# Layer 0's weighted sums over the keys: four column tiles of 32 instead of two of 64

## The chip, the cores and the metric

The kernel runs on one core of one Trainium2 chip. The metric is the device time of one execution in microseconds (us). Five engines of the core take part: TensorE (PE in the profile; its weight loads are listed apart as PEld), VectorE (DVE), ScalarE (ACT), GpSimd (POOL) and SyncE (SP), which issues most of the DMA transfers.

## The reference

The input x has 8 images of 512 channels and 32 x 32 = 1024 positions. Two attention layers follow each other. The core of layer 0, cut to what matters here:

```
h = group_norm(x);  q, k, v = split(qkv_w @ h + qkv_b)          # 8 heads of 64 channels
q, k, v = fake_quant(q), fake_quant(k), fake_quant(v)            # one 8-bit scale for each whole tensor
w = softmax(einsum('bct,bcs->bts', q * scale, k * scale))        # 64 head-images, 1024 x 1024
a = einsum('bts,bcs->bct', w, v)                                 # weighted sums over the keys s
x = x + proj_w @ a + proj_b
```

Layer 1 is a group norm and an attention with a single head of 512 channels on the result, with projections wq, wk, wv and wp, and again a residual sum.

## The kernel before

**First stage (0 to about 600 us).** Image by image the kernel normalises x, multiplies it with the qkv weights and writes q, k and v to device memory, because the quantization needs the extremes of the whole tensors before any score can be computed.

**Second stage (about 600 us to the end).** Layer 0's attention is a generator, `attention()`. Its work is cut into 512 *units* (b, j, hf, s): image b, pair of heads j, half hf of the 1024 queries (512 each), key tile s of 128 keys. What a unit passes through:

- `scores(u)`: two matmuls, one for each head of the pair, give the scores of 128 keys against 512 queries in a two-bank PSUM tile `st`. Each has a contraction of 64 channels, so the two heads share the array by rows (64*128 in the profile). ACT takes the exponential into `pt`.
- `split(u)`: `pt` (32-bit) is split into two 16-bit parts, `two[:, 0]` (a cast, on ACT or POOL) and `two[:, 1]` (the rest, by a subtraction on DVE). Sums over both parts are close to 32-bit sums.
- `over_keys(us)`: the weighted sums, `av` in the profile. The stationary operand is v of the unit's key tile, 128 keys x 128 channels, of which 64 belong to each head of the pair; the moving operand is a part of the exponentials, 128 keys x 512 queries, for each head. The result for a pair is one PSUM bank `av`, head 0 in partitions 0 to 63 and head 1 in 64 to 127, accumulated over the 8 key tiles and both parts.
- `totals(us)`: the row sums, `sm` in the profile, with a stationary operand of ones, 128 x 32 (`ones16`). Four matmuls for a unit (two parts x two heads) write four partition strips of 32 of one PSUM bank, strips of `QUAD` = 32.

For image 0 every fourth key tile is an exception (`plain(b, s)`): its exponentials stay 32-bit, and `over_keys` and `totals` multiply them in two and two 32-bit matmuls. That is 16 units of the 512.

A step of the generator, `advance()`, takes four units through `over_keys` and `totals` and calls `scores` for four later ones. The order inside the step has three forms. The usual one is `over_keys` of four units and then `totals` of the four. A `dense` step does two units at a time: `over_keys`, `totals`, `scores`, `over_keys`, `totals`. A `late` step is similar, with `scores` between the first `over_keys` and `totals`. The rest of the work (the projection of layer 0, `pj`; layer 1's products `g`, `v2ps`, `s`, `o`) comes from a second generator, `others()`, which calls `advance()` at its own places. In the second stage all matmuls pass through `mm`, which chains each to the one before, so PE runs in program order:

```
part = lhsT.shape[-1] / P if lhsT.shape[-1] in (32, 64) else 1.0
...
pe.t += math.prod(rhs.shape[1:]) * 1.677e-3 * part
```

The same helper advances the planner's clock `pe.t`. From the planner's estimates the order of the chores on DVE and ACT is set when the program is built. A matmul with 32 stationary columns counts half of one with 64.

Each step of `over_keys` and `totals` keeps its PSUM bank in the pool `ps_v` (two banks): one `av` and one `sm`. `finish` copies both out on ACT after the last key tile of a half.

Of the kernel before, what the change touches and what calls it, by code (L numbers as in the profile page):

```python
# [58 lines left out]
def attn_pair_kernel(  # L59
# [101 lines left out]
    def awaits(t):  # L161

        pe.t = max(pe.t, t + 0.1)
# [41 lines left out]
    def mm(ps, lhsT, rhs, **kw):  # L205
        ins = nc.tensor.matmul(ps, lhsT=lhsT, rhs=rhs, **kw).ins  # L206
        part = lhsT.shape[-1] / P if lhsT.shape[-1] in (32, 64) else 1.0
        if rhs.dtype in (BF, F16, F32R):
            part *= 0.25 * lhsT.shape[0] / P
        pe.t += math.prod(rhs.shape[1:]) * 1.677e-3 * part  # L210
        if last_mm[0] is not None:
            tc.add_manual_dep(ins, last_mm[0].name, IN_ORDER, reason="order")
        last_mm[0] = ins
# [90 lines left out]
    with ExitStack() as fast:  # L304
# [4 lines left out]
        def av_bank(name):  # L309
            return ps_v.tile([P, 512], F32, tag="v", name=name)  # L310
# [447 lines left out]
        HALF = (slice(0, CH), slice(CH, P))  # L758

        QUAD = P // 4  # L760
# [33 lines left out]
        def plain(b, s):  # L794
            return b == 0 and s % 4 == 3
# [54 lines left out]
        def attention():  # L850
# [8 lines left out]
            pts, parts, avs, sms, rss, ready = {}, {}, {}, {}, {}, {}  # L859
# [57 lines left out]
            def need(u):  # L917

                while u not in ready:
                    e, name = (act, "cast") if u not in at_hand else (dve, "sum")  # L920
                    e.begin(next(i for i, c in enumerate(e.chores) if c[0] == name))

            def over_keys(us):
                need(us[-1])
                awaits(ready[us[-1]])
                pe.t += 0.12
                for u in us:
                    b, j, hf, s = units[u]
                    if s == 0:
                        avs[b, j, hf] = av_bank(f"av_{b}_{j}_{hf}")  # L930
                    if plain(b, s):
                        for i, r in enumerate(HALF):
                            mm(
                                avs[b, j, hf][r, :], lhsT=vfs[j][:, s // 4, r],
                                rhs=parts[u][:, i, :], start=False, stop=(s == NT - 1),
                            )
                        continue
                    for w in range(2):
                        for i, r in enumerate(HALF):
                            mm(  # L940
                                avs[b, j, hf][r, :], lhsT=pairs[b, j][2][:, s, r],
                                rhs=parts[u][:, w, i, :], start=(s == 0 and w == 0),
                                stop=(s == NT - 1 and w == 1),
                            )

# [61 lines left out]
            for u in range(0, len(units), 4):  # L1007
                b, j, hf, s = units[u]
# [17 lines left out]
                if late:  # L1026
                    over_keys((u, u + 1))
                    two(scores, u + 6)
                    totals((u, u + 1))
                    over_keys((u + 2, u + 3))  # L1030
                    totals((u + 2, u + 3))
                    two(split, u + 6)
                    two(scores, u + 8)
                elif dense:
                    over_keys((u, u + 1))
                    totals((u, u + 1))
                    two(split, u + 6)
                    two(scores, u + 8)
                    over_keys((u + 2, u + 3))
                    totals((u + 2, u + 3))  # L1040
                else:
                    over_keys(range(u, u + 4))
                    totals(range(u, u + 4))
                    two(split, u + 6)
                    two(scores, u + 8)
# [995 lines left out]
```

## Time and profile before

| | |
|---|---|
| Median of 3 runs | 2625.35 us (2622.46 to 2626.37) |
| The profiled execution's own time | 2624.97 us |
| Its span, first to last instruction | 2623.2 us |
| Mean granted TensorE clock | 0.995 |
| Busy: PE, PEld, DVE, ACT, POOL | 97%, 67%, 71%, 53%, 7% of the span |
| PE busy in 740 to 2408 us of the span | 1652.44 of 1668 us |
| `av` in 16-bit: matmuls, weight loads | 1984, 1984 |
| `sm` in 16-bit: matmuls, weight loads | 1984, 1984 |

The span leaves out what lies before the first and after the last instruction, 1.8 us here. The profile models the ends of matmuls, and matmuls overlap: a 16-bit one with 512 columns is listed with a duration of about 380 ns, while the next one on the same columns of the array starts after 216 ns. The time that a group of matmuls takes from the array is therefore read from where it starts to where the next group starts. In the profile a shape like 128*64 gives the rows and the columns of the array that a matmul occupies.

### The profile page before, as it was taken

Reading aid. Unit: us, or ns where it says so; the run is one execution under the profiler, and the core shown is the slowest. Engines: PE = TensorE matmul, PEld = TensorE weight load, DVE = VectorE, ACT = ScalarE, POOL = GpSimd, SP = SyncE. Lnnn points to the kernel's source line nnn. Section 1 sums busy time; section 2 is a strip of 40 time slices with the busy share of each in tenths; the row PEclk is TensorE's granted clock in tenths of the full one; section 3 lists DMA queues with packets and bytes.
Section 4 is the critical chain, followed back from the end, with each engine's and each line's share of the span. In section 5 each row is a group of like instructions: output and inputs, shape, how many; then the busy total and the mean of one; then the engine's idle time right before and its main releaser. Section 6 shows DMA issues by size and latency. Waiting matters only on the chain.

```text
span 2623.2 us, 34796 instructions
## 1 busy us (share of the span) xinstructions
PE 2556.4 (97%) x13686; PEld 1755.6 (67%) x13686; DVE 1864.0 (71%) x2675; ACT 1390.1 (53%) x1750; POOL 193.4 (7%) x160
## 2 busy tenths in 40 slices
PE   7899999998989999999999999999999999999998
PEld 4788888882236765775677576757766775677687
DVE  7866666558767777877776777778777776776544
ACT  3333333326866674766566566746665665664121
POOL 0000000001210001000100010010001000100000
PEclk9999999999999999999999999999999999999999
DMA  4433233333311123223212322322232123212211
GB/s 172 149 121 117 108 114 128 121 129 105 130 66 53 58 93 113 63 76 108 94 46 77 121 90 61 101 83 84 80 106 94 52 77 117 85 45 82 93 37 38
DMA packets 154942, 241.79 MB, mean 92 GB/s; under 512 B 26512, under 2 KB 92048, under 8 KB 153232
## 3 DMA queue, kind: packets, MB, share of 16 engines
q1 hardware_dynamic: 124064, 181.50, 21.0%
q10 hardware_dynamic: 30704, 57.97, 6.5%
q8 instruction: 109, 1.79, 0.3%
q14 instruction: 65, 0.53, 0.1%
HBM read 152.59 MB, written 86.28 MB: 91 GB/s over the span
## 4 chain that ended last, share of the span: by engine, by line
PE 87%; DVE 6%; issue 2%; ACT 2%; DMA 2%; POOL 0%; ACTq 0%; SPq 0%; DVEq 0%; POOLq 0%
PE s L206 15%; PE o L206 14%; PE qkps L206 13%; PE pj L206 8%; PE av L206 8%; PE v2ps L206 7%; PE vps L206 7%; PE g L206 7%; PE st L206 4%; PE sm L206 4%; DVE two L91 1%; ACT pt L91 1%; DMA raw<-q_d 1%; PE fold L206 0%; DVE acc L91 0%
## 5 line engine op out<-in xcount | busy, mean ns | idle before, releaser
L91 ACT ACTIVATE pt<-st,esc 128x1024 f32<-128x1024 f32 x496 | 526.9, 1115 | 356.6 <-PE st L206 331.7
L91 DVE TENSOR_TENSOR two<-pt,two 128x1024 f16<-128x1024 f32 x496 | 598.3, 1222 | 139.8 <-POOL two L906 111.0
L91 ACT CAST two<-pt 128x1024 f16<-128x1024 f32 x358 | 362.3, 1055 | 9.0 <-issue 6.5
L906 POOL CAST two<-pt 128x1024 f16<-128x1024 f32 x128 | 167.9, 1312 | 1557.0 <-PE sm L206 1036.0
L206 PE MATMUL av<-two,v 128*64 128x512 f16 x1984 | 246.1, 383 | 0.2 <-DVE two L91 0.2
L206 PE MATMUL s<-g,h 128*128 128x256 f32 x1024 | 234.1, 381 | 0.0
L206 PE MATMUL pj<-ao,wp 128*128 128x512 f32 x512 | 223.6, 595 | 0.0
L206 PEld LDWEIGHTS s<-g,h 128*128 128x128 f32 x1024 | 192.8, 190 | 31.9 <-issue 4.3
L206 PEld LDWEIGHTS <-v 128*64 128x64 f16 x1984 | 98.2, 109 | 133.9 <-issue 66.4
L206 PE MATMUL st<-q,k 64*128 64x512 bf16 x1024 | 162.0, 382 | 23.2 <-ACT pt L91 12.0
L206 PE MATMUL s<-g,sums 128*128 128x256 f32 x768 | 178.4, 381 | 0.2 <-DVE p L91 0.2
L206 PEld LDWEIGHTS pj<-ao,wp 128*128 128x128 f32 x512 | 96.1, 190 | 121.3 <-issue 114.1
L206 PE MATMUL o<-p,v 128*128 128x256 f32 x768 | 175.2, 382 | 1.0 <-DVE p L91 1.0
L206 PEld LDWEIGHTS o<-p,v 128*128 128x128 f32 x768 | 144.3, 190 | 27.1 <-issue 5.7
L206 PEld LDWEIGHTS s<-g,sums 128*128 128x128 f32 x768 | 144.7, 190 | 24.2 <-issue 4.6
L206 PE MATMUL sm<-two,ones 128*32 128x512 f16 x1984 | 137.8, 383 | 1.0 <-ACT rs L91 1.0
L91 ACT ACTIVATE u_ring<-qkps,qkbt 128x512 f32<-128x512 f32 x89 | 60.9, 685 | 140.9 <-PE qkps L206 131.2
L206 PE MATMUL qkps<-half,w_high 128*128 128x512 f32 x480 | 130.5, 394 | 0.0
L206 PEld LDWEIGHTS <-k 64*128 64x128 bf16 x1024 | 33.9, 94 | 143.4 <-issue 139.2
L206 PE MATMUL qkps<-half,w_mix 128*128 128x512 f32 x480 | 129.5, 392 | 0.0
L206 PE MATMUL qkps<-half,w_low 128*128 128x512 f32 x480 | 129.4, 391 | 0.0
L206 PE MATMUL g<-h,wa 128*128 128x256 f32 x512 | 120.6, 383 | 1.6 <-DVE h L91 1.6
(209 smaller groups left out, 3854.1 us busy)
## 6 DMA issues: line engine op xcount, KB each, us to landing
rs<-rs_d SPq DMA_DIRECT2D x80, 256.0 KB
x<-in_x_dram SPq DMA_DIRECT2D x32, 512.0 KB
q_d<-wa SPq DMA_DIRECT2D x32, 512.0 KB
k_d<-wa SPq DMA_DIRECT2D x32, 512.0 KB
raw<-q_d SPq DMA_DIRECT2D x32, 512.0 KB
raw<-k_d SPq DMA_DIRECT2D x32, 512.0 KB
v_d<-v_ring SPq DMA_DIRECT2D x32, 512.0 KB
x_d<-h SPq DMA_DIRECT2D x64, 256.0 KB
```

Source lines behind the costliest of these rows:

```text
L91: ins = self.latest = op(*args, **kw).ins
L206: ins = nc.tensor.matmul(ps, lhsT=lhsT, rhs=rhs, **kw).ins
L906: copy(two[:, 0], pt)
```

## The change

In `over_keys`, the loop over the two halves of the pair's 128 channels becomes a loop over four quarters of 32 channels. Quarters 0 and 1 belong to head 0, quarters 2 and 3 to head 1, so the moving operand of quarter i is `parts[u][:, w, i // 2, :]`. Each quarter writes its own strip of 32 partitions of the same bank. The path of the 16 `plain` units is untouched, and so are `totals` and `scores`.

```
                     for w in range(2):
-                        for i, r in enumerate(HALF):
+                        for i in range(4):
+                            r = slice(i * QUAD, (i + 1) * QUAD)
                             mm(
                                 avs[b, j, hf][r, :], lhsT=pairs[b, j][2][:, s, r],
-                                rhs=parts[u][:, w, i, :], start=(s == 0 and w == 0),
+                                rhs=parts[u][:, w, i // 2, :], start=(s == 0 and w == 0),
                                 stop=(s == NT - 1 and w == 1),
                             )
```

`av` then has 3968 16-bit matmuls of 128*32 and as many weight loads, where it had 1984 of 128*64. For the planner nothing changes in sum: four times a quarter is two times a half. PE's program grows by 3968 instructions, and the order of the instructions on DVE and ACT differs in a handful of neighbouring places; on SP and POOL it is the same.

## The prediction

> **What bounds the kernel now.** I began with the busy shares in the stretch in which layer 0's attention of images 1 to 7 runs among the other products, 740 to 2408 us, as the windows view has it (span, then busy us and count of each engine, clock, DMA share, GB/s):
>
> ```profile
> 740.00:2408.00 1668.00, 1652.44 (x9540) 1098.70 (x9539) 1247.14 (x1578) 1036.32 (x1288) 154.20 (x117) 1.00 0.25 81
> ```
>
> PE is idle for 1668.00 - 1652.44 = 15.6 us, under 1%. DVE has a quarter to spare and ACT over a third. So PE's own order of matmuls is the time here, and what it takes from the array can be saved. The chain that ended last agrees: the page gives PE 87% of it. In the costliest groups (count, then busy us and mean ns of one) the two that matter are
>
> ```profile
> L206 PE MATMUL av<-two,v 128*64 128x512 f16 x1984 | 246.1, 383 | 0.2 <-DVE two L91 0.2
> L206 PE MATMUL sm<-two,ones 128*32 128x512 f16 x1984 | 137.8, 383 | 1.0 <-ACT rs L91 1.0
> ```
>
> Same count, same moving size, same mean, and yet `sm` fills little over half the time of `av`: four `sm` matmuls run side by side, and two of `av`. Per matmul `av` costs 246.1 / 1984 = 124 ns and `sm` 69 ns. If the change only doubled the count at 69 ns, `av` would take 3968 x 69 ns = 276 us, 30 us more. Whether that reading holds is the question, so I went to the chain in order of time (start us, us, what), once through a dense step and once through a usual one:
>
> ```profile
> 1000.15 0.98 PE av L206 x8
> 1001.13 0.55 PE sm L206 x8
> 1001.68 0.54 PE st L206 x4
> ...
> 1032.82 0.54 PE st L206 x4
> 1033.36 1.85 PE av L206 x16
> 1035.20 0.98 PE sm L206 x16
> 1036.18 0.54 PE st L206 x4
> ```
>
> Call *wave* the matmuls that run side by side: two of `av` or `st`, four of `sm`. Eight more `av` matmuls, four waves, cost 1.85 - 0.98 = 0.87 us, so a wave is 0.217 us. Eight more `sm` matmuls, two waves, cost 0.98 - 0.55 = 0.43 us, 0.215 us a wave. I use 0.216. What is left of a group is the same for both: 0.98 - 4 x 0.216 = 0.116 us for `av`, 0.55 - 2 x 0.216 = 0.118 for `sm`, 0.108 for `st`. Every group pays some 0.115 us whatever its length. That fixed part, not dearer waves, is why short `sm` groups average 69 ns.
>
> Is the fixed part paid for a new bank, for new data, or for a new division of the array? Image 0 answers, in the timeline of PE (start us, us with overlaps, then the form):
>
> ```profile
> 656.82 0.62 PE L206 MATMUL av<-two,v 128*64 128x512 f16 x4
> 657.28 1.02 PE L206 MATMUL av<-aside,vf 128*64 128x512 f32 x4
> 658.23 0.40 PE L206 MATMUL sm<-two,ones 128*32 128x512 f16 x4
> 658.46 1.02 PE L206 MATMUL sm<-aside,ones 128*32 128x512 f32 x4
> ```
>
> From 16-bit to 32-bit operands at an unchanged 128*64, two waves last 657.28 - 656.82 = 0.46 us, and the single wave of `sm` 0.23: a wave each and no more than 0.03 over. `st` also passes from one PSUM tile to another inside its four matmuls, two waves in 0.54 with the one fixed part at its end. So neither data, type nor bank costs it; the change of tile shape does.
>
> **What the Trainium skill says.** "TensorEngine Tiling (Array Packing)", section "Tiling Modes", lists 128x64 as two tiles and 128x32 as four, and says that changing the mode, not just the tile, drains TensorE. The trace agrees, with the 0.115 us. "TensorE: Matmul & The Clock Gate", Part 3, "The mechanism", says that a weight load overlaps running matmuls only where the row group differs; the trace disagrees, for `av` and `sm` reload their columns for every matmul, with all 128 rows, at 0.216 us a wave. The same page, "Wait — 56ns, not 53.3ns?", gives some 62 ns per matmul for a sequencer that decodes in software. No long stretch here shows whether that applies; I price it as a rival.
>
> **The change part by part.**
>
> *Waves.* A unit has 2 parts x 2 halves = 4 matmuls in 2 waves before, and 2 x 4 = 8 matmuls in 2 waves after. 3968 / 4 = 1984 / 2 = 992 waves, at the same 0.216 us: 0. The cover is the array's column tiles; bounds: 0 if they run as `sm`'s do, and the feeding rival below if not. A gain per wave has no source.
>
> *Weight loads.* 1984 more, each of 32 columns and not 64. They lie under the wave before, as `sm`'s loads do (PEld idles between groups). Only the first of a group is bare, and it loads fewer columns: 0 to 0.015 us of gain a group, taken at 0.
>
> *Changes of shape.* I counted in the order of PE's program. For images 1 to 7 the 448 units stand in 89 groups of four and 46 of two, 135 `av` groups. 129 are followed directly by `sm`; in the 6 late steps an `sm` is followed by `av`. At these 135 places both sides become 128*32 and the fixed part goes. The change into `av` from `st` (64*128) stays, and the one from `sm` to `st`. 135 x 0.115 = 15.5 us less.
>
> *Image 0.* The first half of its 16 steps loses a fixed part. The second half gains one, as the 32-bit `av` stays 128*64 and stands behind a 16-bit `av` of 128*32: 16 x (-0.115 + 0.115) = 0. Nor is PE the limit there: its chain of waits from 640 to 670 us is mostly DVE's `two` and the DMAs of `raw` and `rs`. Bounds: -2 to +2 us.
>
> *Semaphores, other engines, queues.* The first matmul that needs `two[:, 1]` stands at the same place, half way through a unit; behind it on PE stand only the rest of `av` and `sm`, which need the same unit. No wait is added. DVE and ACT keep their order but for a few neighbours during image 0; no DMA or copy is added, and SP and POOL stay as they are. The planner's `pe.t` gets 4 x 1/4 for 2 x 1/2: 0.
>
> *What of it reaches the end.* PE is the path for nearly all of 740 to 2408 us, so I carry the 15.5 us through. Late next would be ACT's exponentials behind `st` and DVE's `two`, but a step is shortened by 0.12 to 0.24 us, 1 to 2% of the 1668 / 112 = 14.9 us from one step to the next, against spare shares of 25% and 38%. The tail from 2408 us holds no attention and only moves earlier.
>
> **Sum.** 0 + 0 - 15.5 + 0 = -15.5 us against the profiled execution's own 2624.97 (span 2623.2 and 1.8 around it): 2609.5 us. That execution stands 0.4 us under the median of the runs shown, 2625.35.
>
> **The rivals.**
>
> *The gain is taken up by waits.* PE comes earlier to places where ACT or DVE are just in time. For it: the chain shows 1.22 us of "issue" and ACT's `pt` near 1050 us. Against: PE waited for `st`'s buffers, the most frequent of its waits, only 10 times and 4.7 us in 740 to 2408 us. Half lost: 2624.97 - 7.8 = 2617 us.
>
> *The change does not do what it says.* If the 0.115 us were the price of a new accumulation group behind it and not of the shape, nothing would be saved: 2625 us. Against it stand image 0's lines.
>
> *Feeding the array (slower).* A wave then needs four matmuls and four weight loads in 0.216 us, 54 ns for a matmul. A group of four units is 32 `av` and 16 `sm` matmuls, 96 instructions at that pace, where before only `sm`'s 16 had it. If each matmul costs the skill's 62 ns, an estimate from that page, a wave takes 0.248: 896 waves of images 1 to 7 x 0.032 = +28.7, less 15.5 = +13, 2638 us. It decides from 15.5 / 896 = 17 ns a wave on, at 58 ns per matmul. For it: no row before shows more than 16 such matmuls in a row, and a queue could cover those. Against it: an `sm` group of 16 keeps 0.215 us to its last wave; and between two steps stand several us of 32-bit products at 381 to 595 ns each[...]. Were the loads of four different slices of v bare, it would be worse still, some 0.1 us a wave (110 ns a load): +90 us. `sm`'s hidden loads speak against that; I leave it outside the range.
>
> **How the numbers follow.** The full gain 0.74 (2606 to 2613), taken up in part 0.10 (to 2620), nothing saved 0.05, slower 0.11. The likeliest gives 2609.5. The range 2605 to 2624 holds the first two with image 0's bounds and a little on each side; left out are the other two cases, 0.16. A measurement of this kernel can tell about 0.2% from no change, some 5 us. Faster by more: 0.74 + 0.10 = 0.84; within: 0.05; slower: 0.11.
>
> **What would show it.** Right: `av` of 128*32 x3968 with busy time close to before, 240 to 250 us; the chain with `av` x32 and `sm` x16 together at 2.71 us where 1.85 + 0.98 = 2.83 stood; `st` groups at 0.54 as before; PE's idle time not grown. Wrong: `av` x32 well over 1.8 us (feeding), or `sm` still beginning 0.1 us late behind `av` (no fixed part saved), or the saved 15.5 us found again as PE's idle time before `st` or `g`.

## The result, and the profile after

The changed kernel takes 2613.83 us (median of 6 runs, 2613.07 to 2615.8) against 2625.86 us before (6 runs, 2622.46 to 2628.64): 12.0 us less, a ratio of 0.9956 with a 95% interval of 0.9943 to 0.9969. The profiled execution took 2613.41 us with a span of 2611.6, 11.6 us less than before's. The forecast was 2609.5 us within 2605 to 2624: the right side, the right mechanism, and a gain about a quarter smaller than worked out.

The costliest groups of the page after (count, busy us, mean ns):

```profile
L206 PE MATMUL av<-two,v 128*32 128x512 f16 x3968 | 244.7, 381 | 0.0
L206 PE MATMUL sm<-two,ones 128*32 128x512 f16 x1984 | 136.2, 379 | 0.6 <-ACT rs L91 0.6
```

These are to be read against 246.1 and 137.8 us. Twice the `av` matmuls fill the same time: the array takes four of them side by side. An average of 69 ns a matmul would have given 276 us.

The chain of waits of the kernel after, through the dense step and the usual step that were shown of before (start us, us, what):

```profile
1000.15 0.98 PE av L206 x16
1001.13 0.43 PE sm L206 x8
1001.56 0.54 PE st L206 x4
...
1032.35 0.54 PE st L206 x4
1032.89 1.84 PE av L206 x32
1034.73 0.86 PE sm L206 x16
```

`av` is as long as it was (0.98 and 1.84 for 0.98 and 1.85), and `sm` is shorter by 0.12 us (0.43 and 0.86 for 0.55 and 0.98). `sm` now lasts 2 x 0.216 and 4 x 0.216 us and nothing else. The chain puts a group's fixed part at the group that follows the change of shape; the one in front of `av` is still there. Together 1.84 + 0.86 = 2.70 us stand where 2.83 stood.

The windows view of the stretch 740 to 2408 us:

```profile
740.00:2408.00 1668.00, 1652.62 (x11396) 1115.71 (x11385) 1253.78 (x1589) 1040.75 (x1296) 156.76 (x117) 1.00 0.26 81
```

PE is idle for 15.4 us, as before (15.6). It is still the engine that sets the time.

**Where the rest of the expected gain went.** The runs of `st`, `av`, `sm` and other products stand in the same order in both kernels, 742 of them. I paired them by place and summed what changed between the start of one and the start of the next. The `s` runs of the fourth line are explained below the table:

| part of the second stage | us |
|---|---|
| images 1 to 7: from `av` to `sm` (129 places), from `sm` to `av` (6) | -14.65, -0.63 |
| images 1 to 7: the rest of `sm`, and `av` before `st` | -0.93, -0.04 |
| images 1 to 7: inside `st`, ahead of other products and ahead of `av` | +1.63, +0.74 |
| images 1 to 7: other products ahead of `st`: seven runs of `s`, and all the others | -0.80, +1.37 |
| images 1 to 7: after `sm`, ahead of other products | +0.08 |
| image 0 | +1.45 |
| what lies ahead of image 0's first `av` | +0.39 |
| after the last `sm` | -0.17 |

The first two lines are the mechanism: -16.25 us, of which 0.36 belong to one place near 1692 us where `av` of the kernel before took that much longer than in other groups of its length; without it they are -15.9. The third line is new: `st` became longer at some places. Of the 21 `st` groups in images 1 to 7 that are longer by some 0.12 us, 13 stand ahead of a product of layer 1 and 8 ahead of `av`. They are the same 21 in a second profile of the changed kernel (after_again, below). The timeline of PE around one of them, before:

```profile
1350.06 1.05 PE L206 MATMUL sm<-two,ones 128*32 128x512 f16 x16
1351.04 0.62 PE L206 MATMUL st<-q,k 64*128 64x512 bf16 x4
1351.59 1.78 PE L206 MATMUL s<-g,sums 128*128 128x256 f32 x7
```

and that of ACT there:

```profile
1348.58 0.63 ACT L91 ACTIVATE p<-p 128x512 f32<-128x512 f32 x1 [1.94 <-DVE p L91]
1349.11 2.10 ACT L91 ACTIVATE pt<-st,esc 128x1024 f32<-128x1024 f32 x2
```

The same two timelines after, PE first:

```profile
1346.89 1.04 PE L206 MATMUL sm<-two,ones 128*32 128x512 f16 x16
1347.86 0.74 PE L206 MATMUL st<-q,k 64*128 64x512 bf16 x4
1348.53 1.78 PE L206 MATMUL s<-g,sums 128*128 128x256 f32 x7
```

and ACT:

```profile
1345.52 0.63 ACT L91 ACTIVATE p<-p 128x512 f32<-128x512 f32 x1 [1.94 <-DVE p L91]
1346.06 2.10 ACT L91 ACTIVATE pt<-st,esc 128x1024 f32<-128x1024 f32 x2
```

Before, ACT finished its two exponentials at 1351.21 us and `st`, begun at 1351.04, lasted 0.55 us: just in time for its second PSUM tile. After, ACT finishes at 1348.16, and `st`, begun at 1347.86, lasts 0.67. PE came 0.12 us earlier in relation to ACT, and waited 0.12 us. The list of waits hardly shows it (`st` behind ACT's `pt`, 740 to 2408 us: 4.7 us before, 5.8 after), for most of these waits hide under the modelled ends of the matmuls ahead of them.

Such a wait is not always lost time. Seven of the 13 stand ahead of a run of 56 `s` matmuls, and each of these runs is 0.11 us shorter than before, again in both profiles. The place just shown is one of the seven. In the middle of its run a weight load needs ACT's copy `kept_u`. Copy and load before:

```profile
1354.48 0.62 ACT L91 COPY kept_u<-s 128x512 f32<-128x512 f32 x1
1355.15 3.32 PEld L206 LDWEIGHTS s<-g,h 128*128 128x128 f32 x16 [0.25 <-ACT kept_u L91]
```

and after:

```profile
1351.30 0.62 ACT L91 COPY kept_u<-s 128x512 f32<-128x512 f32 x1
1351.97 3.33 PEld L206 LDWEIGHTS s<-g,h 128*128 128x128 f32 x16
```

In both kernels the load begins 0.05 us behind the copy and 4.11 us behind the start of `st`. Before, its matmul stood ready and began together with it, at 1355.15. After, PE has already lost 0.12 us at `st`, and the load stands 0.12 us ahead of its matmul, which begins at 1352.09. ACT held PE up here in both kernels; the wait only moved from `s` to `st`. So 14 of the 21 places took back the gain of their step: 2.37 - 0.80 = 1.6 us.

The +1.37 us in the other products is mostly in runs that begin with `g` (1.17 us, at five places). The second profile of the changed kernel has 1.21 us there too, but at six places of which only three are the same (and near 789 us a wait of 1.7 us that both other profiles have is gone). What holds `g` up is left open.

### The profile page after: what moved, and what is told of

The parts are those of the page before. It is cut to its first block, busy times and chain, and to the rows that moved or that the text cites. A ratio compares the mean times of both kernels' runs of the same rounds, so it can differ in the third digit from the quotient of the medians.

```text
span 2611.6 us, 38765 instructions
## 1 busy us (share of the span) xinstructions
PE 2546.6 (98%) x15670; PEld 1763.3 (68%) x15670; DVE 1863.7 (71%) x2675; ACT 1389.8 (53%) x1750; POOL 195.3 (7%) x160
## 4 chain that ended last, share of the span: by engine, by line
PE 88%; DVE 4%; ACT 3%; issue 2%; DMA 1%; POOL 0%; SPq 0%; ACTq 0%; DVEq 0%; POOLq 0%
PE s L206 15%; PE o L206 13%; PE qkps L206 13%; PE pj L206 9%; PE av L206 8%; PE v2ps L206 7%; PE vps L206 7%; PE g L206 7%; PE st L206 4%; PE sm L206 4%; ACT pt L91 1%; PE fold L206 1%; DVE two L91 1%; DVE acc L91 1%; ACT aside L91 1%
## 5 line engine op out<-in xcount | busy, mean ns | idle before, releaser
L206 PE MATMUL av<-two,v 128*32 128x512 f16 x3968 | 244.7, 381 | 0.0
L206 PEld LDWEIGHTS <-v 128*32 128x32 f16 x3968 | 91.2, 96 | 136.3 <-issue 63.4
```

## The experiments

| kernel | median us | ratio to before, 95% |
|---|---|---|
| before (24 runs in the end) | 2625.07 | |
| changed kernel | 2613.83 | 0.9956 (0.9943 to 0.9969) |
| the same once more | 2614.43 | 0.9957 (0.9943 to 0.9971) |
| split_group | 2625.6 | 1.0006 (0.9998 to 1.0014) |
| alternate | 2700.39 | 1.0284 (1.0265 to 1.0303) |
| img0_halves | 2614.81 | 0.9958 (0.9944 to 0.9971) |
| plain_quads | 2614.19 | 0.9956 (0.9942 to 0.9969) |
| p_later | 2613.35 | 0.9953 (0.9939 to 0.9967) |
| p_later_before | 2625.17 | 0.9999 (0.9990 to 1.0007) |
| no_dense | 2625.07 | 0.9999 (0.9991 to 1.0008) |

Each ratio is to the runs of the kernel before that were there at the time: 6 for the changed kernel, 17 (median 2625.46 us) for split_group to plain_quads, 24 for the others.

### Four tiles without fewer changes: split_group

```
-                        for i in range(4):
-                            r = slice(i * QUAD, (i + 1) * QUAD)
+                        n = 4 if u >= us[len(us) // 2] else 2
+                        for i in range(n):
+                            r = slice(i * P // n, (i + 1) * P // n)
...
-                                rhs=parts[u][:, w, i // 2, :], start=(s == 0 and w == 0),
+                                rhs=parts[u][:, w, i * 2 // n, :], start=(s == 0 and w == 0),
```

> Within every group of weighted sums the first half of the units keeps two tiles of 64 and the second half takes four of 32. Half of all av waves now run in four tiles, but the array changes its shape inside the av group instead of behind it: 745 changes of shape in the second stage against 739 before and 604 after. Theory (only the number of changes counts, at about 0.115 us each): as before, 2626 us plus 6 x 0.115 = 0.7. Rival (four tiles are themselves cheaper, for example by their smaller weight loads): half of the gain, about 2620 us.

Measured: 2625.6 us, as before. The chain of waits of this kernel, in the usual step:

```profile
1031.69 1.96 PE av L206 x24
1033.65 0.86 PE sm L206 x16
```

`sm` has its short form, and `av`, half of it in two tiles and half in four, is longer by the same 0.11 us: 1.96 + 0.86 = 2.82 us, as in the kernel before. The fixed part moved into `av` with the change of shape. So four tiles are worth nothing by themselves here; the gain is that of the missing change.

### Many more changes: alternate

The same edit with `n = 4 if w == 1 else 2`.

> Within every unit the waves of the first 16-bit part run in two tiles of 64 and those of the second part in four of 32, so that the array changes its shape at every wave of av: 1435 changes against 739 before, 696 more. Theory: each costs what a removed one gave, 0.115 us, of which the first wave's bare weight load is part: 696 x 0.115 = 80 us more than before, about 2706 us; a little less if image 0 hides its share of 64. Rival (the 0.11 us belongs to the end of an accumulation group or to the passage to another PSUM bank): no change, 2626 us, for neither is added.

Measured: 2700.39 us (2 runs), 75 us over before: 75 / 696 = 0.108 us a change. The rival, no change in the time, is out. The chain of waits in a usual step:

```profile
1046.81 2.66 PE av L206 x24
1049.48 0.86 PE sm L206 x16
```

2.66 + 0.86 = 3.52 us against 2.83 before, for six more changes: 0.115 us each, the price read before the prediction. Over the whole kernel it comes out a little lower than 80 us because the slower PE waits less: the same pairing of groups gives 3.1 us in images 1 to 7 and 3.8 us in image 0 that `st` ahead of `av` no longer waited.

### Image 0: img0_halves and plain_quads

The edit of img0_halves is the same loop with `n = 4 if b > 0 else 2`; plain_quads takes the changed kernel and gives the 32-bit `av` matmuls four tiles too:

```
                     if plain(b, s):
-                        for i, r in enumerate(HALF):
+                        for i in range(4):
+                            r = slice(i * QUAD, (i + 1) * QUAD)
...
-                                rhs=parts[u][:, i, :], start=False, stop=(s == NT - 1),
+                                rhs=parts[u][:, i // 2, :], start=False, stop=(s == NT - 1),
```

> Image 0 keeps two tiles of 64 for all its weighted sums, images 1 to 7 have four of 32. Theory (image 0 lost 1.5 us with the change, because a 32-bit av of 128*64 now stands behind a 16-bit one of 128*32 and pays a change and a bare weight load, while DVE and the transfers limit that stretch anyway): 1.5 us less than after, about 2612.3 us. Rival (the 1.5 us is a shift of waits from run to run): 2613.8 us as after.

> Image 0's 32-bit weighted sums run in four tiles of 32 as well. This takes 32 more changes of shape out of image 0's stretch (572 in all against 604), with the bare 64-column load: on PE 16 x (0.09 + 0.054) + 16 x 0.1 = 3.9 us. Theory: image 0 is not limited by PE throughout, so between the 1.5 us that it had lost and these 3.9: 2610 to 2612.3 us. Rival (32-bit matmuls don't run side by side four times with different weights as they do two times): 16 units x 2 waves dearer, over 2614 us.

Measured: 2614.81 and 2614.19 us, neither better than the changed kernel's 2613.83 and 2614.43. The first is a miss: in the profile of img0_halves image 0's stretch is 1.38 us shorter than in that of the changed kernel, as expected, but what lies ahead of it is 0.57 us longer and images 1 to 7 take 1.26 us more. Differences of that size come and go: images 1 to 7 gained 13.2 us in the first profile of the changed kernel and 14.7 in the second. Image 0's 1.4 us can be read in its stretch, but not in the kernel's time.

The second missed its expectation too, and its 2614.19 us is what the rival named. But the rival's reason is out: paired with the changed kernel, the 32-bit groups and the changes around them in image 0 take 3.7 us less, close to the 3.9 that were worked out, so the 32-bit matmuls do run four side by side. Image 0's stretch is 0.6 us longer all the same: `sm` behind `av` waits 2.7 us more, nearly all at one place, and 1.6 us more go ahead of `st` and inside it. Waits of PE in image 0's stretch of plain_quads (us in total, times, longest):

```profile
PE st L206 <- ACT aside L91: 7.0, 14, 0.6
PE sm L206 <- ACT rs L91: 3.2, 1, 3.2
```

The second line was 1.0 us in the kernel before and 0.6 in the changed one. Its chain can be seen in the timeline of plain_quads:

```profile
718.28 1.28 DVE L91 SCALAR_TENSOR_TENSOR ao<-ao,scl,rs 128x1024 f32<-128x1024 f32 x1 [3.70 <-DMA rs<-rs_d]
...
719.60 0.58 ACT L91 COPY rs<-sm 128x512 f32<-128x512 f32 x1 [2.54 <-DVE ao L91]
...
720.24 1.04 PE L206 MATMUL sm<-two,ones 128*32 128x512 f16 x8 [3.21 <-ACT rs L91]
```

The next `sm` needs a PSUM bank, which ACT empties into the tile `rs`; ACT waits for DVE's division, the last reader of that tile; and DVE waits for the transfer that brings the inverse row sums back. PE reaches this place earlier and stands there longer, in this execution.

### The waits of st: p_later and p_later_before, with after_again

In layer 1's `s_block` the exponential on the sums `p` becomes a chore, and is settled ahead of its readers:

```
                 there = dve.do(elements(512), lambda: tt(dst, ps, u, ALU.add))
-                exp(dst, dst, there + 0.1)
+                act.later(
+                    "pexp", 0.62, lambda: act.activation(dst, dst, AF.Exp, scale=SM1),
+                    there + 0.1, 5.0,
+                )
                 if i == 1:
+                    act.settle("pexp")
...
             def whole(ps):
+                act.settle("pexp")
```

> The changed kernel once more, beside the three that follow, so that differences of 2 to 3 us between them can be told on one chip: 2613.8 us as before.

> The changed kernel, with the exponentials of layer 1's sums p on ACT no longer put where they are written down, but handed to the planner as chores with a due time, so that ACT can take layer 0's two exponentials of st first. In the trace of the changed kernel 22 second halves of st waited for ACT, 20 of them for 0.12 us more than before. Theory (the 3 us that images 1 to 7 gave back were waits of st behind a p exponential on ACT): most of these waits go, 1.5 to 3 us less than the changed kernel, 2611 to 2612.3 us. Rival (they are set by ACT's pace as a whole, or by DVE's): no change, 2613.8 us.

> The same edit of ACT's order on the kernel before, with two tiles of 64. Theory: in the kernel before st had almost no wait at these places, so the edit brings 0 to 1 us there, about 2625.5 us; the distance to p_later is then that of the changes of shape alone, 135 x 0.12 = 16 us less image 0's 1.5, about 14 us, instead of 12. Rival (the order of the p exponentials has nothing to do with what was given back): the distance stays at 12 us.

Measured: 2614.43 us for the changed kernel, 2613.35 for p_later, 2625.17 for p_later_before. The timeline of PE in p_later, at the place shown above:

```profile
1345.73 1.04 PE L206 MATMUL sm<-two,ones 128*32 128x512 f16 x16
1346.70 0.61 PE L206 MATMUL st<-q,k 64*128 64x512 bf16 x4
1347.23 1.99 PE L206 MATMUL s<-g,sums 128*128 128x256 f32 x8
```

and of ACT:

```profile
1343.95 2.12 ACT L91 ACTIVATE pt<-st,esc 128x1024 f32<-128x1024 f32 x2 [1.53 <-PE st L206]
1345.95 0.63 ACT L91 ACTIVATE p<-p 128x512 f32<-128x512 f32 x1
```

ACT takes `pt` first, and `st` lasts 0.53 us again. Over the kernel, `st` ahead of other products is 1.77 us shorter than in after_again, so the 13 waits ahead of these products did come from the place of the `p` exponential in ACT's order; the 8 ahead of `av` stay. But the products that lie ahead of `st` are 2.89 us longer. In 0.88 of it the wait came back at the place from which it had moved: the seven runs of `s` are as long again as in the kernel before. Another 1.71 us is at three other runs of `s` (1.04 at one), where neither profile of the changed kernel has a delay. The waits of PE from 740 to 2420 us have, in p_later,

```profile
PE s L206 <- DVE p L91: 1.1, 3, 0.8
```

against 0.2 us at one place in after_again. The total moves by 1 us at most, with ranges that overlap (2612.37 to 2614.39 against 2612.49 to 2614.53), and the distance between the two p_later kernels is 11.8 us, not 14. The wait was removed, and the time was not. Whether ACT's new order also made those three waits for DVE is open: there is one profile of p_later, and two executions of the changed kernel differ by 1.86 us in the same part.

### Fewer changes elsewhere: no_dense

```
-                elif dense:
+                elif dense and b == 0:
```

> The changed kernel, with the 17 dense steps of images 1 to 7 in the usual order (all weighted sums, then all row sums, then scores). That takes out 18 further changes of shape (586 against 604). Theory (a change of shape costs 0.11 us wherever it stands and PE is the path): 18 x 0.11 = 2 us less, 2611.8 us. Rival (dense steps are there because scores have to come earlier; later scores make PE wait for the exponentials): 2614 to 2618 us.

Measured: 2625.07 us, 11 us slower than the changed kernel, with 18 changes fewer. The longest waits of PE from 740 to 2390 us (us in total, times, longest):

```profile
PE pj L206 <- ACT pt L91: 11.9, 12, 1.0
PE av L206 <- DVE two L91: 6.9, 1, 6.9
```

The projection `pj`, in these steps, takes its PSUM from the pool of `st`. Behind the usual order it follows `scores` directly and waits for the exponential that empties the bank, 1 us at each of 12 places; the waits of `st` for the same exponentials shrink in return, from 7.1 us in after_again to 0.3. A saved change of shape is 0.11 us; each wait of `pj` costs nine of them. The wait of 6.9 us is a single one, at 791 us in image 1. Image by image, images 2 to 7 take 1.0 to 1.5 us each more than in after_again, and image 1 takes 4.3 us more.

## Why the prediction was right, step by step

- **Waves at 0: right.** `av` fills 244.7 us for 246.1, and a group of 32 takes 1.84 us for 1.85. The feeding rival would have begun to decide at 17 ns a wave and nothing of it is seen: 48 matmuls and 48 weight loads of `av` and `sm` ran in 2.70 us.
- **The fixed part belongs to the change of shape: right**, shown by split_group (the change kept, nothing gained) and alternate (696 changes added, 75 us lost). The rival that the change does not do what it says is out.
- **135 x 0.115 = 15.5 us: right**, 15.9 us by the paired groups (16.25 with the one longer stop of the kernel before). At the median it is 0.110 us where `sm` follows `av` and 0.010 in the rest of `sm`, whose first wave now lasts 0.216 us for 0.226: 0.12 for 0.115 at a place.
- **Image 0 at 0: mis-sized**, +1.45 us, inside the stated bounds of 2. The new change costs more than the removed one gave. The likely reason, not tested by itself, is that the 32-bit `av` behind it starts with a bare load of 64 columns. The timeline of PE in the kernel after has it:

```profile
657.91 0.61 PE L206 MATMUL av<-two,v 128*32 128x512 f16 x8
658.46 1.08 PE L206 MATMUL av<-aside,vf 128*64 128x512 f32 x4
659.46 0.40 PE L206 MATMUL sm<-two,ones 128*32 128x512 f16 x4
```

  The 16-bit `av` lasts 0.55 us for 0.46, the 32-bit one 1.00 for 0.95. Summed, 2.31 us are added and 2.21 saved (0.34 of it a single wait of `sm` that was shorter in this execution); the rest is `st`, which waits 1.4 us longer, in this stretch mostly for ACT. The second profile of the changed kernel has +1.43 us for image 0.
- **All of it reaches the end: this step failed in size.** The text looked at shares of busy time (25% and 38% to spare) and at the list of waits (4.7 us in 10 waits). Neither tells how many places are *just* in time. There are about three in each image, 21 in all, and "`st` groups at 0.54 as before" did not hold there. At 14 of them the 0.12 us of the step was lost, 1.6 us together; at the other seven the wait moved to `st` from the `s` behind it. A further 1.4 us went in other products, most of it in `g`. The rival "taken up by waits" was thus true, but for 1.6 us, or 3.0 with the other products, where it had put 7.8; and the places are others than the one near 1050 us that it named.

The terms in order: -16.25 + 2.37 - 0.80 + 1.37 + 0.08 + 1.45 + 0.39 - 0.17 = -11.56, which is the 11.6 us between the two spans.

## What to carry to other kernels

Count the changes of the array's tile shape along PE's order and price one by the difference between a group's length and its waves; where two neighbouring groups can use one shape, the change between them can go, here at no cost to the waves (0.216 us in both shapes). Before carrying a small gain on a saturated engine through to the end, look for the places where a partner is just in time, in the order of starts and not in the list of waits: in these traces each such place took back at most the gain of its own step, and nothing where the partner had held the engine up a little later anyway. Where an order looks wasteful in changes, ask first which buffer it keeps apart.

## What the runs showed of the hardware

A wave of 512 columns in 16 bits takes 0.216 us with two column tiles and with four, with one set of weights for all tiles or a different one for each. The pace of 96 weight loads and matmuls in 2.70 us, 28 ns each, held to the last wave. Between such stretches stand slower 32-bit products, so what a longer stretch at this pace would do is not shown.

A change of tile shape cost 0.108 us (696 of them added) to 0.115 us (six in one step). In the traces the first weight load behind a change starts only 2 ns ahead of its matmul. How much of the price is the array's change and how much is this load, no run here separates.
